# Where the products of a step stand between scores and sums, and when their outputs are turned, in the first pass of a two-layer attention kernel

## Chip, cores and metric

One core of one Trainium2 chip. The metric is the device time of one execution in microseconds (us), of which the median of several runs is given. All data are 32-bit floats.

## What is computed

Two layers on x of shape 8 x 256 x 64 x 64. The first is attention with keys and values from a 4x4 strided convolution (so 4096 queries against 256 keys, 8 heads of 32), the second linear attention over q, k, v and a 5x5 depthwise copy of them. The part that matters here, cut from the reference:

```
xr = layernorm(conv4x4_stride4(x, w_sr));  q = w_q x;  k, v = split(w_kv xr)
attn = softmax(q k^T * 32**-0.5)           # per head, over 256 keys
x2 = x + gamma * w_out (attn v)            # end of layer 0
qkv = w_qkv x2                             # layer 1 starts: 768 x 256 on 4096 columns
...                                        # depthwise 5x5, relu attention, projection
```

## The kernel before, in words

The kernel has three passes: the first computes layer 0 and the qkv of layer 1 and stores them to DRAM, the second the sums and the 5x5 branch, the third the output. Only `first_pass` (L575) changes.

**Steps.** The first pass is a loop over n (L991) of 256 steps and some more that empty the pipeline. A step is one (image b, strip s of 512 columns, half c of the heads, half kc of the keys): 32 steps an image, 4 a strip. With m = n - 1, a step n holds for TensorE:

- `scores` (L770) of n: four products, one a head, each on 32 rows of the array ("32x512" in the profile, line L774), into four PSUM banks. ScalarE takes each out with an exponential (L780) into a tile `e`.
- `valued` (L786) of m: four products on 32 columns of the array (L791) of `e` with the values, into the bank `av`.
- after both key halves, so in even n, `counted` (L804): four products of ones with the sum of the two halves' `e` (L807), into the bank `den`. The sum of the halves is made by GpSimd (POOL) in `joined` (L800, L802): four additions in odd n, **in place over the `e` of the first half**. They therefore wait until `valued` of that first half, which stands in the same odd step, has read it; and `counted` in the step after waits for all four.
- in even n, `queries` (L756): the q of the next two steps (two products of the full array, L759); `normed` (L809): `att` times the reciprocal of `den`, by two transposes on VectorE (DVE), and on ScalarE two checks over 512 columns each, which write back to the bank `den` (L823, L824).
- in steps 12 to 25 of an image, parts of `keys_values` (L675) of the next image (`ahead`): two taps of the convolution a step (L687), then the layernorm and k and v.
- what `todo` holds for n: `added` (L827: the output projection of a strip, L831, and its sum into x, L832, in n = 2 and 6 modulo 8), `differences` (L841, n = 2 modulo 8), and the products of `qkv` (L860).

**The products of qkv.** A pair of strips is done with seven products instead of eight (Strassen-Winograd) for each of three pairs of weights, in the order 1, 2, 0: p1, p2, p6, p7, p4, p5, p3, 21 in 8 steps, one bank each. In the steps 3, 4, 5, 6, 7, 0, 1 modulo 8 there are 4, 3, 4, 0, 3, 4, 3 of them. `ended` (L882) makes an output of a product on DVE (`part_whole`, L891); for pairs 1 and 2 it then transposes it at once (`turned`, L894) and, for pair 1, copies it on ScalarE to `stage` (L893). For pair 0 the sum goes straight to `stage` (L888). `stored` (L899) sends both to DRAM through SP's queue.

**Banks.** Scores, q, the output projection and the qkv products share five banks (`bank`, L591). A scores step takes four of them, in turn, so its last three wait until the three products that stand fourth, third and second ahead of it have been taken out of their banks, mostly by DVE. `av`, `den` and the convolution have a bank each.

**Order.** Every engine runs its instructions in one order, which a planner sets when the program is built: it goes by the order of the code, but puts a later instruction first where it holds the earlier one not ready at that time. `tc.keep_in_program_order` pins an instruction behind all that was traced for its engine before it. Each product of the code becomes two TensorE instructions.

Of the kernel before, what the change touches and what calls it, by code (L numbers as in the profile page):

```python
# [27 lines left out]
F32 = mybir.dt.float32  # L28
AF = mybir.ActivationFunctionType
ALU = mybir.AluOpType  # L30
AX = mybir.AxisListType

P = 128
# [541 lines left out]
def first_pass(ctx: ExitStack, tc: tile.TileContext, a, fine, planes, x2d, kd, vd, wtd):  # L575
# [207 lines left out]

    sums = {}

    def valued(b, s, c, kc, es):  # L786
        if kc == 0:
            sums["av"] = psum_early.tile([P, QB], F32, tag="av", name=f"av_{b}_{s}_{c}")
        for h in range(4):
            cols = slice(h * D0, (h + 1) * D0)  # L790
            nc.tensor.matmul(  # L791
                sums["av"][cols],
                vvs[b][:, kc, c * P + h * D0 : c * P + (h + 1) * D0],
                es[h],
                start=(kc == 0),
                stop=(kc == 1),
            )
# [11 lines left out]
    def normed(b, s, c):  # L809
        av, den = sums["av"], sums["den"]  # L810
        i = 2 * ((b * NG + s) * 2 + c)
        att = rest.tile([P, QB], F32, tag="att", name=f"att_{b}_{s}_{c}", bufs=4)
        r = rest.tile([P, NB, D0], F32, tag="rden", name=f"rden_{b}_{s}_{c}", bufs=1)
        one = two.tile([P, NB], F32, tag="one", name=f"one_{b}_{s}_{c}")
        nc.scalar.copy(att, av)

        nc.vector.transpose(r.rearrange("p n d -> p (n d)"), den)
        nc.vector.reciprocal(one, r[:, :, 0])
        r = rest.tile([P, NB, D0], F32, tag="rall", name=f"rall_{b}_{s}_{c}", bufs=1)
        nc.vector.transpose(r, one.unsqueeze(2).to_broadcast([P, NB, D0]))  # L820
        r = r.rearrange("p n d -> p (n d)")
        nc.vector.tensor_mul(att, att, r)
        nc.scalar.activation(den, den, AF.Copy, accum_out=seen[:, i : i + 1])  # L823
        nc.scalar.activation(den, r, AF.Copy, accum_out=seen[:, i + 1 : i + 2])  # L824
        return att

    def added(b, s, att, oc):  # L827
# [23 lines left out]
        quarters[b, g] = b11, b21, b22, t1, t2, t3, t4  # L851

    def new_stage(b, g, j):
        st = rest.tile([P, 4, NB + 1, NB + 1], F32, tag=f"stage{j}", name=f"stage_{b}_{g}_{j}", bufs=1)
        nc.gpsimd.memset(st[:, :, 0 if g // 2 else NB], 0.0)
        nc.gpsimd.memset(st[:, :, :, 0 if g % 2 else NB], 0.0)
        return st


    def qkv(b, g, pair):  # L860
        js = 2 * pair, 2 * pair + 1
        b11, b21, b22, t1, t2, t3, t4 = quarters[b, g]
        w = consts["wqkv"].rearrange("p c (j r o) -> p c j r o", j=3, r=2)[:, :, pair]
        s1, s2, s3, s4 = (combined[:, pair, i] for i in range(4))
        name = f"{b}_{g}_{pair}"
        stages = [new_stage(b, g, j) for j in js] if pair < 2 else None
        turned = None
        if pair:
            turned = [
                rest.tile([P, NB // 2, 4, D0], F32, tag=f"turned{j}", name=f"turned_{b}_{g}_{j}", bufs=1) for j in js  # L870
            ]

        def product(i, w, x):
            ps = bank(f"qkv_{name}_{i}")
            nc.tensor.matmul(ps, w, x, start=True, stop=True)  # L875
            return ps

        def part(i, bufs=1):
            return halves.tile([P, QB], F32, tag=f"part{i}", name=f"part_{name}_{i}", bufs=bufs)


        def ended(r, h, u, ps, op=ALU.add):  # L882
            if stages:
                y, x = g // 2, g % 2
                inside = stages[r][:, 2 * h : 2 * h + 2, y : y + NB, x : x + NB]
            rows = lambda t: t.rearrange("p (f y x) -> p f y x", f=2, y=NB)
            if not turned:
                nc.vector.tensor_tensor(inside, rows(u), rows(ps), op)  # L888
                return
            whole = part("whole", 2)  # L890
            nc.vector.tensor_tensor(whole, u, ps, op)  # L891
            if stages:
                nc.scalar.copy(inside, rows(whole))  # L893
            nc.vector.transpose(  # L894
                turned[r][:, :, 2 * h : 2 * h + 2].rearrange("p y f e -> p f y e"),
                whole.rearrange("p (f y e) -> p f y e", f=2, y=NB // 2),
            )

        def stored(r):  # L899
            j = js[r]  # L900
            if stages:
                nc.sync.dma_start(
                    planes[b, j].rearrange("g (k i f) e -> g k i (f e)", k=4, i=D1)[:, g],
                    stages[r].rearrange("p f y x -> p (f y x)"),
                )
            if not turned:
                return
            for k in range(4):
                n, src = 4 * (j % 2) + k, turned[r][k * D0 : (k + 1) * D0].rearrange("p y f e -> p y (f e)")
                if j < 4:  # L910
                    dst = kd[b][n].rearrange("a (y w) x b e -> a b (w x) y e", w=2)
                    nc.sync.dma_start(dst[g // 2, g % 2], src)
                else:
                    dst = vd[b][n][1 : NB2 + 1, 1 : NB2 + 1]
                    dst = dst.rearrange("(y w a) (x b) e -> a b w x y e", w=2, a=2, b=2)
                    for w in range(2):
                        nc.sync.dma_start(dst[g // 2, g % 2, w], src[w * NB : (w + 1) * NB])


        u = {}  # L920

        def p1():
            ps = product(1, w[:, 0, 0], b11)
            u[1] = part(1)
            nc.scalar.copy(u[1], ps)

        def p2():
            ended(0, 0, u[1], product(2, w[:, 1, 0], b21))

        def p6():  # L930
            u[2] = part(2)
            nc.vector.tensor_add(u[2], u[1], product(6, s2, t2))

        def p7():
            u[3] = part(3)
            nc.vector.tensor_add(u[3], u[2], product(7, s3, t3))

        def p4():
            ended(1, 0, u[3], product(4, w[:, 1, 1], t4), ALU.subtract)

        def p5():
            ps = product(5, s1, t1)
            ended(1, 1, u[3], ps)
            u[4] = part(4)
            nc.vector.tensor_add(u[4], u[2], ps)
            stored(1)

        def p3():
            ended(0, 1, u[4], product(3, s4, b22))
            stored(0)  # L950

        return [p1, p2, p6, p7, p4, p5, p3]

# [16 lines left out]
    q, es, att = {0: first}, {}, {}  # L970
    ahead = iter(())

    def outputs(b, s):
        return [lambda oc=oc: added(b, s, [att[b, s, 0], att[b, s, 1]], oc) for oc in range(2)]

    def qkv_lazy(b, g, pair):
        made = []

# [9 lines left out]

    n_all = len(order)
    todo = {}  # L990
    for n in range(n_all + 14):  # L991
        m = n - 1
        if n < n_all:
            b, s, c, kc = order[n]
            es[n] = scores(b, s, c, kc, q[n // 2])
        if 0 <= m < n_all:
            valued(*order[m], es[m])
            if order[m][3] == 1:
                counted(*order[m][:3], es.pop(m - 1))
                es.pop(m)  # L1000
                att[order[m][:3]] = normed(*order[m][:3])
        if n < n_all and kc == 1:
            joined(es[n - 1], es[n])
        if n < n_all and kc == 0 and n + 2 < n_all:
            q.pop(n // 2 - 1, None)
            q[n // 2 + 1] = queries(*order[n + 2][:3])
        if n >= 6 and (n - 6) % 8 == 4 and (n - 6) // 4 < B * NG:

            b, s = (n - 6) // 4 // NG, (n - 6) // 4 % NG
            work = [outputs(b, s) + [lambda b=b, s=s: differences(b, s // 2)]]  # L1010
            products = [p for pair in (1, 2, 0) for p in qkv_lazy(b, s // 2, pair)]
            for i in (4, 3, 4, 0, 3, 4, 3):
                work.append(products[:i])
                products = products[i:]
            for i, w in enumerate(work):
                todo.setdefault(n + i, []).extend(w)
        elif n >= 6 and (n - 6) % 8 == 0 and (n - 6) // 4 < B * NG:
            todo.setdefault(n, []).extend(outputs((n - 6) // 4 // NG, (n - 6) // 4 % NG))
        next(weights, None)
        if n < n_all:  # L1020
            b, at = n // 32, n % 32
# [2 lines left out]
            if b + 1 < B:  # L1024
# [6 lines left out]
                    next(ahead)  # L1031
                elif at >= 20:
                    next(ahead, None)
        for f in todo.pop(n, ()):
            f()
    for _ in weights:
        pass

# [3 lines left out]
    total = bank("total")[:, :2]  # L1042
    nc.tensor.matmul(total, mean_w, both, start=True, stop=True)
    fits = const.tile([P, 4], F32, tag="fits", name="fits")
    nc.vector.tensor_scalar(fits[:, 0:1], total[:, 0:1], SUM_MAX / C, None, ALU.is_le)
    nc.vector.tensor_scalar(fits[:, 1:2], total[:, 1:2], INVERSE_MAX / C, None, ALU.is_le)
    nc.vector.tensor_mul(fits[:, 2:3], fits[:, 0:1], fits[:, 1:2])
    nc.vector.tensor_copy(fine, fits[:, 2:3])

# [674 lines left out]
```

## Time and profile before

| what | value |
|---|---|
| median of 10 runs | 4056.96 us (4053.03 to 4063.7) |
| time of the profiled execution | 4055.02 us |
| its span, first to last instruction | 4053.2 us |
| last scores product of the first pass | starts at 2118.68 us |
| TensorE (PE) busy in the span | 3982.0 us, 98% |
| DVE / ScalarE / GpSimd busy | 2261.3 / 1645.5 / 1275.1 us |
| granted TensorE clock | 0.993 of full speed |

The timeline of the trace gives for each row its start, its length, the engine, the line, the operation, the tiles (written <- read), and in brackets how long the engine was idle before it and what ended that. TensorE's matmuls overlap, so their lengths add to more than the time; the distance from one start to the next is what a product takes.

### The profile page before, as it was taken

What the parts mean: (1) busy time and instruction counts of PE and PEld (TensorE: products, weight loads), DVE (VectorE), ACT (ScalarE), POOL (GpSimd) and SP (SyncE); (2) the same over time, 40 slices, a digit from 0 to 9 for tenths busy, and PEclk for the clock granted to TensorE, in tenths of its full rate; (3) what the DMA queues carried; (4) which work ended last, traced back from release to release, by engine and by line L of the source; (5) the groups of instructions that cost most, each with busy time, mean ns of one, the idle gap of its engine ahead of it and who ended that gap; (6) DMA issues with size and microseconds to landing.
All of it is one profiled execution on the core that took longest, in us unless ns stands there. A gap on an engine that the chain in (4) does not pass through costs nothing. (4 is left out here: it accounts for less than half of the span.)

```text
span 4053.2 us, 70276 instructions
## 1 busy us (share of the span) xinstructions
PE 3982.0 (98%) x27074; PEld 2316.2 (57%) x27074; DVE 2261.3 (56%) x3752; ACT 1645.5 (41%) x3473; POOL 1275.1 (31%) x1394
## 2 busy tenths in 40 slices
PE   8999999999999999999998999999999998999999
PEld 4443434434334344343336888888888886556555
DVE  2576455564655545546665566666666665444443
ACT  3345354453544544535552222222222223454444
POOL 2234333343332433423443444434434441000000
PEclk9999999999999999999999999999999999999999
DMA  7655445445354453544549878778777656777674
GB/s 239 189 179 159 125 97 143 100 97 152 91 143 104 98 135 103 136 109 103 135 102 244 246 226 233 220 224 233 220 223 234 204 171 174 232 199 233 196 235 137
DMA packets 569897, 691.37 MB, mean 171 GB/s; under 512 B 60112, under 2 KB 429264, under 8 KB 565328
## 3 DMA queue, kind: packets, MB, share of 16 engines
q1 hardware_dynamic: 569552, 686.78, 60.7%
q8 instruction: 215, 3.52, 0.4%
q14 instruction: 130, 1.06, 0.1%
HBM read 412.54 MB, written 274.10 MB: 169 GB/s over the span
## 5 line engine op out<-in xcount | busy, mean ns | idle before, releaser
L802 POOL TENSOR_TENSOR e<-e,e 128x512 f32<-128x512 f32 x512 | 658.1, 1318 | 938.8 <-PE av L791 923.4
L780 ACT ACTIVATE e<-sc 128x512 f32<-128x512 f32 x1024 | 532.8, 601 | 709.0 <-PE sc L774 709.0
L774 PE MATMUL sc<-q,kk 32*128 32x512 f32 x2048 | 418.5, 640 | 7.2 <-DVE part_whole L891 3.9
L1180 PE MATMUL cv<-w,c 128*128 128x128 f32 x3072 | 385.7, 279 | 6.8 <-POOL c L1124 6.8
L1180 PEld LDWEIGHTS cv<-w,c 128*128 128x128 f32 x3072 | 359.9, 192 | 36.3 <-issue 28.8
L1547 DVE TENSOR_TENSOR y<-z,xs 128x256 f32<-128x256 f32 x256 | 142.6, 645 | 313.6 <-ACT z L1538 295.3
L1222 PE MATMUL sums<-vq,r 128*32 128x288 f32 x4096 | 306.6, 412 | 0.0
L891 DVE TENSOR_TENSOR part_whole<-part,qkv 128x512 f32<-128x512 f32 x256 | 170.7, 670 | 219.9 <-PE qkv L875 216.1
L774 PEld LDWEIGHTS sc<-q,kk 32*128 32x128 f32 x2048 | 130.0, 183 | 278.0 <-issue 140.3
L875 PE MATMUL qkv<-differences,combined 128*128 128x512 f32 x576 | 278.6, 592 | 0.8 <-DVE differences L848 0.8
L1196 ACT ACTIVATE r<-s 128x512 f32<-128x512 f32 x256 | 160.5, 627 | 291.8 <-DVE s L1195 288.3
L791 PE MATMUL av<-e,vv 128*32 128x512 f32 x2048 | 275.5, 608 | 0.0
L1538 ACT ACTIVATE z<-p,bn 128x256 f32<-128x256 f32 x256 | 133.9, 578 | 315.0 <-PE p L1529 208.5
L759 PE MATMUL q<-x,wq 128*128 128x512 f32 x512 | 255.3, 621 | 0.0
L1184 PE MATMUL cv<-c,w 128*128 128x128 f32 x2048 | 253.4, 277 | 0.0
L1529 PE MATMUL p<-att,wproj 128*128 128x512 f32 x512 | 249.4, 609 | 1.9 <-ACT att L1512 1.9
L1187 ACT COPY both<-cv 128x512 f32<-128x512 f32 x128 | 75.1, 586 | 432.7 <-PE cv L1180 374.3
L687 PE MATMUL sr<-x,wsr 128*128 128x256 f32 x1024 | 236.9, 385 | 11.5 <-DMA wsr<-in_w_sr_dram 11.5
L1529 PE MATMUL p<-agg,wproj 128*128 128x512 f32 x512 | 241.3, 594 | 0.0
L1184 PEld LDWEIGHTS cv<-c,w 128*128 128x128 f32 x2048 | 239.7, 192 | 0.0
L687 PEld LDWEIGHTS sr<-x,wsr 128*128 128x128 f32 x1024 | 192.8, 191 | 76.5 <-issue 40.2
L831 PE MATMUL o<-att,wout 128*128 128x512 f32 x512 | 231.8, 593 | 0.0
(143 smaller groups left out, 6202.3 us busy)
## 6 DMA issues: line engine op xcount, KB each, us to landing
vq<-v SPq DMA_DIRECT2D x256, 384.0 KB
planes<-stage SPq DMA_DIRECT2D x128, 578.0 KB
d<-planes SPq DMA_DIRECT2D x128, 578.0 KB
raw<-planes SPq DMA_DIRECT2D x128, 272.0 KB
x<-in_xp_dram SPq DMA_DIRECT2D x64, 512.0 KB
wsr<-in_w_sr_dram SPq DMA_DIRECT2D x128, 256.0 KB
x<-x SPq DMA_DIRECT2D x128, 256.0 KB
k<-turned SPq DMA_DIRECT2D x256, 128.0 KB
```

Source lines behind the costliest of these rows:

```text
L687: nc.tensor.matmul(ps[:, oc], w[:, ci, oc * P : (oc + 1) * P], xt[:, ci, f * NK : (f + 1) * NK], start=(f == ci == oc == 0), stop=(f == R ...
L759: nc.tensor.matmul(ps, consts["wq"][:, ci, c * P : (c + 1) * P], x_tiles[b][:, ci, s * QB : (s + 1) * QB], start=(ci == 0), stop=(ci == 1),)
L774: nc.tensor.matmul(scs[h], kks[b][rows, c, kc * P : (kc + 1) * P], qs[rows], start=True, stop=True)
L780: nc.scalar.activation(e, scs[h], AF.Exp, scale=D0**-0.5)
L791: nc.tensor.matmul(sums["av"][cols], vvs[b][:, kc, c * P + h * D0 : c * P + (h + 1) * D0], es[h], start=(kc == 0), stop=(kc == 1),)
L802: nc.gpsimd.tensor_tensor(es0[h], es0[h], es1[h], ALU.add)
L831: nc.tensor.matmul(ps, consts["wout"][:, c, oc * P : (oc + 1) * P], att[c], start=(c == 0), stop=(c == 1))
L875: nc.tensor.matmul(ps, w, x, start=True, stop=True)
L1180: nc.tensor.matmul(out, x, m, start=(da == 0), stop=(da == 1))
L1184: nc.tensor.matmul(out, m, x, start=(da == 0), stop=(da == 1))
L1222: nc.tensor.matmul(ps[h * D0 : (h + 1) * D0, : 36 * D1].rearrange("p (r n e) -> p r n e", r=3, e=D1), kt[:, par, h, 2 * r + c], vq[:, r : ...
L1529: nc.tensor.matmul(ps.rearrange("p (f q n) -> p f q n", f=4, q=4), wproj[:, j, oc * P : (oc + 1) * P], src, start=(j == 0), stop=(j == 3),)
```

## The change

1. **Turns a step later.** In `ended` the transpose and the copy to `stage` are put in a list `late`, and so is `stored` for pairs 1 and 2. The list is run in the next step, after that step's `scores`, and its instructions are pinned to the order of the code. `whole` gets 6 buffers instead of 2.
2. **Checks.** In `normed` the two 512-column checks become two 16-column ones, over the column `turn[:, :, 0]` and over `one`, also run late; they no longer write to `den`. The two limits are divided by 32 to match.
3. **Order in a step.** `added` and `differences` come behind `queries` and `normed`, in the step in which they were. The products of qkv come ahead of `queries`. In odd steps except 13 to 25 of an image (`last`) they come **ahead of `valued`**, directly behind `scores`; in the others behind `valued` and `counted`, and the convolution's part comes after them.
4. **Counts.** The products in steps 3, 4, 5, 6, 7, 0, 1 modulo 8 are 2, 3, 4, 1, 4, 3, 4.
5. **Tiles.** `stage` has two slots for four tiles (tag `j % 2`).

The core of the diff:

```
-            whole = part("whole", 2)
+            whole = halves.tile([P, QB], F32, tag="whole", name=f"whole_{name}_{r}_{h}", bufs=6)
             nc.vector.tensor_tensor(whole, u, ps, op)
-            if stages:
-                nc.scalar.copy(inside, rows(whole))
-            nc.vector.transpose(
...
+            def turn():
+                tc.keep_in_program_order(
+                    nc.vector.transpose(
...
+                if stages:
+                    tc.keep_in_program_order(nc.scalar.copy(inside, rows(whole)))
+
+            late.append(turn)
...
+        def ready(r):
+            if turned:
+                late.append(lambda: stored(r))
+            else:
+                stored(r)
...
-        nc.scalar.activation(den, den, AF.Copy, accum_out=seen[:, i : i + 1])
-        nc.scalar.activation(den, r, AF.Copy, accum_out=seen[:, i + 1 : i + 2])
+
+        def noted():
+            for k, t in enumerate((turn[:, :, 0], one)):
+                copy = two.tile([P, NB], F32, tag="copy", name=f"copy_{b}_{s}_{c}_{k}")
+                tc.keep_in_program_order(
+                    nc.scalar.activation(copy, t, AF.Copy, accum_out=seen[:, i + k : i + k + 1])
+                )
+
+        late.append(noted)
...
-        st = rest.tile([P, 4, NB + 1, NB + 1], F32, tag=f"stage{j}", name=f"stage_{b}_{g}_{j}", bufs=1)
+        st = rest.tile([P, 4, NB + 1, NB + 1], F32, tag=f"stage{j % 2}", name=f"stage_{b}_{g}_{j}", bufs=1)
...
             es[n] = scores(b, s, c, kc, q[n // 2])
+        was, late[:] = list(late), []
+        for f in was:
+            f()
+
+
+        last = n < n_all and kc == 1 and not 12 <= n % 32 <= 25
+        if last:
+            for f in todo.pop(n, ()):
+                f()
         if 0 <= m < n_all:
             valued(*order[m], es[m])
             if order[m][3] == 1:
                 counted(*order[m][:3], es.pop(m - 1))
                 es.pop(m)
-                att[order[m][:3]] = normed(*order[m][:3])
-        if n < n_all and kc == 1:
-            joined(es[n - 1], es[n])
+        for f in todo.pop(n, ()):
+            f()
         if n < n_all and kc == 0 and n + 2 < n_all:
             q.pop(n // 2 - 1, None)
             q[n // 2 + 1] = queries(*order[n + 2][:3])
...
+        if 0 <= m < n_all and order[m][3] == 1:
+            att[order[m][:3]] = normed(*order[m][:3])
+        if n < n_all and kc == 1:
+            joined(es[n - 1], es[n])
+        if n >= 6 and (n - 6) % 4 == 0 and (n - 6) // 4 < B * NG:
             b, s = (n - 6) // 4 // NG, (n - 6) // 4 % NG
...
+                for i, count in enumerate((2, 3, 4, 1, 4, 3, 4)):
+                    todo[n + 1 + i] = products[:count]
+                    products = products[count:]
         next(weights, None)
...
-        for f in todo.pop(n, ()):
-            f()
```

More of the change, by code (lines that the diff above doesn't have):

```diff
@@ L784, in first_pass @@
     sums = {}
+    late = []
     def valued(b, s, c, kc, es):
@@ L812, in normed @@
         att = rest.tile([P, QB], F32, tag="att", name=f"att_{b}_{s}_{c}", bufs=4)
-        r = rest.tile([P, NB, D0], F32, tag="rden", name=f"rden_{b}_{s}_{c}", bufs=1)
+        turn = rest.tile([P, NB, D0], F32, tag="rden", name=f"rden_{b}_{s}_{c}", bufs=1)
         one = two.tile([P, NB], F32, tag="one", name=f"one_{b}_{s}_{c}")
         nc.scalar.copy(att, av)
-        nc.vector.transpose(r.rearrange("p n d -> p (n d)"), den)
-        nc.vector.reciprocal(one, r[:, :, 0])
+        tc.keep_in_program_order(nc.vector.transpose(turn.rearrange("p n d -> p (n d)"), den))
+        nc.vector.reciprocal(one, turn[:, :, 0])
         r = rest.tile([P, NB, D0], F32, tag="rall", name=f"rall_{b}_{s}_{c}", bufs=1)
@@ L876, in product, with part @@
             return ps
-        def part(i, bufs=1):
-            return halves.tile([P, QB], F32, tag=f"part{i}", name=f"part_{name}_{i}", bufs=bufs)
+        def part(i):
+            return halves.tile([P, QB], F32, tag=f"part{i}", name=f"part_{name}_{i}", bufs=1)
         def ended(r, h, u, ps, op=ALU.add):
@@ L889, in ended @@
                 return
-            whole = part("whole", 2)
+            whole = halves.tile([P, QB], F32, tag="whole", name=f"whole_{name}_{r}_{h}", bufs=6)
             nc.vector.tensor_tensor(whole, u, ps, op)
-            if stages:
-                nc.scalar.copy(inside, rows(whole))
-            nc.vector.transpose(
-                turned[r][:, :, 2 * h : 2 * h + 2].rearrange("p y f e -> p f y e"),
-                whole.rearrange("p (f y e) -> p f y e", f=2, y=NB // 2),
-            )
+            def turn():
+                tc.keep_in_program_order(
+                    nc.vector.transpose(
+                        turned[r][:, :, 2 * h : 2 * h + 2].rearrange("p y f e -> p f y e"),
+                        whole.rearrange("p (f y e) -> p f y e", f=2, y=NB // 2),
+                    )
+                )
+                if stages:
+                    tc.keep_in_program_order(nc.scalar.copy(inside, rows(whole)))
+            late.append(turn)
         def stored(r):
@@ L945, in p5 @@
             nc.vector.tensor_add(u[4], u[2], ps)
-            stored(1)
+            ready(1)
         def p3():
             ended(0, 1, u[4], product(3, s4, b22))
-            stored(0)
+            ready(0)
         return [p1, p2, p6, p7, p4, p5, p3]
@@ L971, in first_pass @@
     ahead = iter(())
-    def outputs(b, s):
-        return [lambda oc=oc: added(b, s, [att[b, s, 0], att[b, s, 1]], oc) for oc in range(2)]
     def qkv_lazy(b, g, pair):
@@ L990, in first_pass @@
     todo = {}
-    for n in range(n_all + 14):
+    for n in range(n_all + 16):
         m = n - 1
@@ L1006, in first_pass @@
             q[n // 2 + 1] = queries(*order[n + 2][:3])
-        if n >= 6 and (n - 6) % 8 == 4 and (n - 6) // 4 < B * NG:
-            b, s = (n - 6) // 4 // NG, (n - 6) // 4 % NG
[L1010 to L1018, printed above, removed]
+        if 0 <= m < n_all and order[m][3] == 1:
[3 more added lines that the diff above has]
+        if n >= 6 and (n - 6) % 4 == 0 and (n - 6) // 4 < B * NG:
+            b, s = (n - 6) // 4 // NG, (n - 6) // 4 % NG
+            for oc in range(2):
+                added(b, s, [att[b, s, 0], att[b, s, 1]], oc)
+            if s % 2:
+                differences(b, s // 2)
+                products = [p for pair in (1, 2, 0) for p in qkv_lazy(b, s // 2, pair)]
+                for i, count in enumerate((2, 3, 4, 1, 4, 3, 4)):
+                    todo[n + 1 + i] = products[:count]
+                    products = products[count:]
         next(weights, None)
@@ L1044, in first_pass @@
     fits = const.tile([P, 4], F32, tag="fits", name="fits")
-    nc.vector.tensor_scalar(fits[:, 0:1], total[:, 0:1], SUM_MAX / C, None, ALU.is_le)
-    nc.vector.tensor_scalar(fits[:, 1:2], total[:, 1:2], INVERSE_MAX / C, None, ALU.is_le)
+    nc.vector.tensor_scalar(fits[:, 0:1], total[:, 0:1], SUM_MAX / D0 / C, None, ALU.is_le)
+    nc.vector.tensor_scalar(fits[:, 1:2], total[:, 1:2], INVERSE_MAX / D0 / C, None, ALU.is_le)
     nc.vector.tensor_mul(fits[:, 2:3], fits[:, 0:1], fits[:, 1:2])
```

## Prediction

> **What bounds the kernel now.** First the page: TensorE is busy for 98% of the span, and the last scores product of the first pass starts at 2118.68 us, so this pass is half the time and is a row of TensorE products without holes of any length. Every wait of TensorE there is time of the kernel; ScalarE, DVE and GpSimd (POOL) at 41, 56 and 31% are paid only where TensorE waits for them.
>
> ```profile
> PE 3982.0 (98%) x27074; PEld 2316.2 (57%) x27074; DVE 2261.3 (56%) x3752; ACT 1645.5 (41%) x3473; POOL 1275.1 (31%) x1394
> ...
> L802 POOL TENSOR_TENSOR e<-e,e 128x512 f32<-128x512 f32 x512 | 658.1, 1318 | 938.8 <-PE av L791 923.4
> ```
>
> The second line is `joined`: 1.3 us an addition, four in two steps, and POOL's wait ahead of them is for `valued` (av). Then the waits of the stretch from 60 to 2120 us, TensorE's weight loads alone, which stand for the products behind them:
>
> ```profile
> PEld sc L774 <- DVE part L945: 47.3, 81, 1.6
> PEld sc L774 <- ACT stage L893: 43.2, 57, 0.8
> ...
> PEld den L807 <- POOL e L802: 30.4, 65, 2.7
> ...
> PEld sc L774 <- DVE part_whole L891: 17.0, 18, 2.0
> PEld sc L774 <- DVE part L932: 15.9, 60, 1.0
> ```
>
> Scores wait for a bank that DVE has still to empty: this is what can be won. Part of a weight load's idle time goes by while products still run, so I size the loss from starts: scores to valued is 1.07 us at the least in the timeline, and what is over that is the wait. In images 2 to 8 it is 0.50, 1.03, 0.50, 1.03 and 0.57 us in the steps 4, 5, 6, 0 and 2 modulo 8 and none in 1, 3, 7: 3.63 us in 8 steps, 101.6 in the 28 such groups, and 108.4 with what is more in steps 22 and 24 of an image. The first image has 25.4, of it 4.8 before its step 11. Sum 133.7 us.
>
> Third, two pieces of the timeline. Steps 37 and 38, as most are:
>
> ```profile
> 356.63 2.17 PE L774 MATMUL sc<-q,kk 32*128 32x512 f32 x8
> ...
> 358.74 1.07 PE L791 MATMUL av<-e,vv 128*32 128x512 f32 x8
> ...
> 359.73 1.98 PE L875 MATMUL qkv<-x,wqkv 128*128 128x512 f32 x4
> ...
> 359.93 4.94 POOL L802 TENSOR_TENSOR e<-e,e 128x512 f32<-128x512 f32 x4 [8.12 <-PE av L791]
> ...
> 361.55 1.88 PE L875 MATMUL qkv<-differences,combined 128*128 128x512 f32 x4
> ...
> 363.36 1.64 PE L774 MATMUL sc<-q,kk 32*128 32x512 f32 x8
> ...
> 364.93 1.07 PE L791 MATMUL av<-e,vv 128*32 128x512 f32 x8
> ```
>
> The first row is a stalled scores step (356.63 to 358.74, 2.11 us). Then valued releases POOL 1.19 us after its start, POOL adds until 364.87, and `counted` can follow valued at 365.81 without waiting: **four qkv products, 3.63 us, cover POOL**. Steps 5 and 6, where there are no qkv products yet:
>
> ```profile
> 77.82 1.06 PE L791 MATMUL av<-e,vv 128*32 128x512 f32 x8
> ...
> 78.82 1.90 PE L774 MATMUL sc<-q,kk 32*128 32x512 f32 x8
> ...
> 79.02 6.46 POOL L802 TENSOR_TENSOR e<-e,e 128x512 f32<-128x512 f32 x4 [5.21 <-PE av L791]
> ...
> 80.65 1.06 PE L791 MATMUL av<-e,vv 128*32 128x512 f32 x8
> ...
> 81.53 1.09 PE L807 MATMUL den<-e,ones_w 128*32 128x512 f32 x4
> ...
> 85.53 1.05 PE L807 MATMUL den<-e,ones_w 128*32 128x512 f32 x2 [1.69 <-POOL e L802]
> 86.50 1.98 PE L759 MATMUL q<-x,wq 128*128 128x512 f32 x4
> ```
>
> Valued, scores, valued, counted with nothing of the full array between: counted takes 4.97 us from its start to the next product instead of 0.97, and q, which needs nothing of POOL, stays behind it: the planner did not move it up. The same is seen in steps 2, 4, 8 and 10.
>
> **What the Trainium skill says.** "TensorEngine Tiling (Array Packing)", Key Properties: changing the tiling mode drains TensorE. The trace agrees: scores to valued (rows to columns) takes 1.07 us, valued to counted (same mode) 0.88. Same page, Gotcha 1 (PSUM Pressure): different row tiles write different banks; here four of five banks a step, hence the waits above. "TensorE: Matmul & The Clock Gate", Part 3, The mechanism: matmuls are not reordered on the engine. Agrees: q stands behind the waiting counted at 86.50.
>
> **The change, part by part.**
>
> *Qkv products ahead of valued in odd `last` steps.* It moves what covers POOL to the wrong side: POOL is released only by valued, and between valued and counted there are now scores and valued alone. From the start of valued: release 1.20 us (358.74 to 359.93), four additions, mean 1293 ns in the steady part (330 to 2115 us), 5.17, then 1.02 from POOL's end to the product behind counted (85.48 to 86.50): 7.39 us. Without a wait it is 1.00 + 1.07 + 0.88 + 0.97 = 3.92. **Wait 3.47 us** a time. Nothing else in those steps can shorten it, since the additions wait for valued alone; behind counted stand, on TensorE, qkv, q, output projection and all later steps. How often: `last` holds in 9 odd steps of an image (1 to 11 and 27 to 31), 72 in all; in steps 1, 3, 5, 7, 9 of the first there is no product to move and the wait is there already. 67 x 3.47 = 232.5, less what four of those places (steps 12, 28, 32, 256) wait already, 0.79 + 1.09 + 0.24 + 1.58 = 3.7: **+229**. In the last image, step 19 has no convolution behind it and only 2 products: about +2. Bounds of a wait: four additions take 4.94 us at best and 5.41 at worst in steady steps, so 3.24 to 3.71.
>
> *Scores free of DVE.* Turns (0.71 us each) no longer stand between the outputs, and behind the last products there is now valued (1.00 us), q (1.8), the convolution (3.45) or the output projection (3.5). DVE needs 0.65 to 0.69 us an output, two for p5, against 0.86 a product: for p7, p4, p5, p3 the last bank needed, p5's, comes free some 4.1 us after the first product starts, while scores begin at 3.5 + 1.0. What is left: step 24 (only 0.55 us between) and the last image's steps 14 to 26, some 8 us; in the first image DVE's weight products (1.9 us each) still stand in the way, of 20.6 I take half. 108.4 - 8 + 10: **-110** (bounds -95 and -125).
>
> *Switches of mode* in a `last` step: before scores-valued-full-scores, after scores-full-valued-scores, three each. Full to columns is not in the trace; nearest 0.1 (full to rows) to 0.2 (rows to columns): 0, between -7 and +7 over 72 steps.
>
> *Small checks.* Away: 0.58 + 0.19 + 0.60 + 0.19 us of ScalarE, 128 times; come: two copies of 16 columns, not shown; from copies of 512 (0.59) and 256 (0.37) columns some 0.15 to 0.25 plus 0.19 each. About 100 us of ScalarE time, hidden by its 59% idle; nobody waits for it: 0. If that cover were gone, 0.8 us a place.
>
> *Turns and stores a step later.* The same instructions; on ScalarE the copies (0.62) come behind the exponentials. On SP each store's one plane and 4 or 8 token DMAs move behind the next step's; queued behind them are x2 stores and convolution weights, for which TensorE waits 5.3 us today. 0, bounds -5 and +10.
>
> *Two `stage` slots.* POOL's memsets wait for the other pair's store. A store issued at 1030.34 lets the memset at 1034.90 go, 4.6 us later; between one pair's store and the other's memset lies at least a step of 8 us. 0, bound +10 (a memset ahead of the additions lengthens the wait above).
>
> **Sum**: 4055.0 (profiled) - 110 + 229 + 2 = 4176; the median lies 1.9 above the profiled time: **4178**. With the bounds (-125 + 214 to -95 + 248, and the small ones) 4140 to 4225.
>
> **Rivals.** (1) *The planner moves full-array products in front of counted*, where it holds POOL late. For it: it does reorder (a convolution tap between two output products in step 50). Against it: it left q behind counted in five steps of the same pattern. Then the wait is covered by qkv and q, and only the gain is left: 4057 - 110 = **3947**, faster. It decides from 3.47 us of work put there; at 1.8 us in all 67 places gain and loss are even. (2) *It moves one product*, 0.86 us: 67 x 2.61 - 3.7 - 110 = +61: **4118**. (3) *The scores' waits stay* because pinned turns now stand at the head of DVE's queue: +229 and no gain, **4288**. Against it: TensorE's new waits give DVE time. (4) Waits and gains cancel otherwise: 4057.
>
> **Chances.** Forecast 0.74, (1) 0.14, (2) 0.06, (3) 0.03, (4) 0.03. Faster by over 0.2% (about what a measurement of this kernel can tell from no change) 0.15; within 0.03; slower 0.82. The forecast's own range with (2) and slack for the planner's order gives 4090 to 4250; outside lie (1), (3) and a little of the forecast.
>
> **What would show it.** Right: scores to valued or to qkv at 1.07 us nearly everywhere; counted to the next product 4.4 us (0.97 + 3.47) in 67 even steps, with POOL named as releaser, 0.97 in steps 14 to 26; waits of counted for POOL about 230 us in all. Wrong: qkv or q products between valued and counted (rival 1 or 2), scores still waiting for DVE (3), waits for DMA in the first pass, or additions much off 1.29 us.

## The result, and the profile after

The changed kernel takes **4182.7 us** (median of 8 runs, 4179.58 to 4187.68) against 4056.9 us before (28 runs): 1.031 times as long, 95% interval 1.0301 to 1.0319. The forecast was 4178. The profiled execution, of 4186.6 us, has a span of 4184.8 us, 131.6 more than before.

The page after, with the lines for TensorE, for the additions of `joined` and for `counted`:

```profile
span 4184.8 us, 70247 instructions
...
PE 4076.1 (97%) x27074; PEld 2309.5 (55%) x27074; DVE 2242.2 (54%) x3752; ACT 1516.8 (36%) x3473; POOL 1271.5 (30%) x1394
...
L804 POOL TENSOR_TENSOR e<-e,e 128x512 f32<-128x512 f32 x512 | 654.3, 1310 | 897.0 <-PE av L793 897.0
...
L809 PE MATMUL den<-e,ones_w 128*32 128x512 f32 x1024 | 333.7, 608 | 35.8 <-POOL e L804 33.8
```

TensorE is busy for 97%, and yet the time is 3% longer: its busy time rose by 94.1 us (3982.0 to 4076.1) with the same 27074 instructions, so much of the waiting counts as busy and this line can't show the loss. The waits of the first pass can (60 to 2245 us; waited for, us in all, times, longest):

```profile
POOL stage L864 <- DMA planes<-stage: 314.9, 80, 14.5
...
PEld den L809 <- POOL e L804: 225.2, 275, 2.6
...
PEld sc L774 <- ACT copy L830: 18.4, 22, 0.8
...
PEld sc L774 <- DVE whole L901: 10.7, 16, 2.5
...
PEld sc L774 <- DVE part L967: 6.3, 7, 3.4
```

Before, the weights of `counted` waited 30.4 us for GpSimd; now 225.2. Those of the scores waited 47.3 and 15.9 us for the two kinds of `part` and 17.0 for `part_whole`; now 6.3 for `part` and 10.7 for `whole`. The 18.4 us put down to the small checks (`copy`, L830) are no loss of that size: ahead of the first weight load of most scores steps stands an idle of some 0.8 us, while products still run. These 22 are the steps 4, 12 and 28 of an image (and step 20 of the last), which lose 0.2 us each by their starts. The timeline of one step with products ahead of `valued`:

```profile
650.74 1.07 PE L793 MATMUL av<-e,vv 128*32 128x512 f32 x8
...
651.74 1.14 PE L774 MATMUL sc<-q,kk 32*128 32x512 f32 x8
651.93 4.96 POOL L804 TENSOR_TENSOR e<-e,e 128x512 f32<-128x512 f32 x4 [11.41 <-PE av L793]
...
652.81 1.06 PE L793 MATMUL av<-e,vv 128*32 128x512 f32 x8
...
653.69 1.85 PE L809 MATMUL den<-e,ones_w 128*32 128x512 f32 x4
...
655.72 1.04 PE L809 MATMUL den<-e,ones_w 128*32 128x512 f32 x2 [0.18 <-POOL e L804]
...
656.95 1.05 PE L809 MATMUL den<-e,ones_w 128*32 128x512 f32 x2 [0.18 <-POOL e L804]
...
657.93 1.12 PE L885 MATMUL qkv<-differences,combined 128*128 128x512 f32 x2
```

Here scores follow `valued` without a wait (652.81 - 651.74 = 1.07), which was the aim. But GpSimd is released by the `valued` at 650.74, 1.19 us after its start, adds until 656.89, and between that `valued` and `counted` TensorE has only scores and one more `valued`. `counted` takes 657.93 - 653.69 = 4.24 us where 0.97 would do.

Summed over the first pass from starts, as in the prediction: "scores' wait" is what a scores group takes beyond 1.07 us until the next group starts, "counted's wait" what `counted` takes beyond 0.97, "pass" the time from the first scores product to the last, "behind" the time from there to the end of the span. A delay of the start of `counted`, or of other products, is in neither column of waits. The columns come from the one profiled execution of each kernel, and executions of one kernel lie up to some 13 us apart (before: 4052.05 to 4064.63), so a few us in them decide nothing. All in us:

| kernel | median | pass | scores' wait | counted's wait | behind |
|---|---|---|---|---|---|
| before | 4056.9 | 2067.0 | 133.9 | 19.9 | 1934.5 |
| after | 4182.7 | 2178.8 | 34.8 | 228.9 | 1952.6 |

So the time went to `counted` (+209.0) and to the stretch behind the last scores (+18.1); the scores gave back 99.1, and the first scores start 1.7 us later.

### The profile page after: what moved, and what is told of

The parts are those of the page before. It is cut to its first block, busy times and chain, and to the rows that moved or that the text cites. A ratio compares the mean times of both kernels' runs of the same rounds, so it can differ in the third digit from the quotient of the medians.

```text
span 4184.8 us, 70247 instructions
## 1 busy us (share of the span) xinstructions
PE 4076.1 (97%) x27074; PEld 2309.5 (55%) x27074; DVE 2242.2 (54%) x3752; ACT 1516.8 (36%) x3473; POOL 1271.5 (30%) x1394
## 3 DMA queue, kind: packets, MB, share of 16 engines
q8 instruction: 215, 3.52, 0.4%
## 5 line engine op out<-in xcount | busy, mean ns | idle before, releaser
L809 PE MATMUL den<-e,ones_w 128*32 128x512 f32 x1024 | 333.7, 608 | 35.8 <-POOL e L804 33.8
L774 PE MATMUL sc<-q,kk 32*128 32x512 f32 x2048 | 324.1, 641 | 4.8 <-DVE part L967 3.0
L885 PE MATMUL qkv<-differences,combined 128*128 128x512 f32 x576 | 304.6, 620 | 1.0 <-DVE differences L857 1.0
L759 PE MATMUL q<-x,wq 128*128 128x512 f32 x512 | 245.3, 601 | 0.0
L767 ACT COPY q<-q 128x512 f32<-128x512 f32 x128 | 75.1, 586 | 457.0 <-PE q L759 457.0
L901 DVE TENSOR_TENSOR whole<-part,qkv 128x512 f32<-128x512 f32 x256 | 175.3, 687 | 121.8 <-PE qkv L885 66.6
```

What stands on the lines that cost most here:

```text
L759: nc.tensor.matmul(ps, consts["wq"][:, ci, c * P : (c + 1) * P], x_tiles[b][:, ci, s * QB : (s + 1) * QB], start=(ci == 0), stop=(ci == 1),)
L774: nc.tensor.matmul(scs[h], kks[b][rows, c, kc * P : (kc + 1) * P], qs[rows], start=True, stop=True)
L809: nc.tensor.matmul(sums["den"][h * D0 : (h + 1) * D0], ones_w, es[h], start=True, stop=True)
```

## Experiments

Twelve kernels. Theory A (the prediction's): full-array products ahead of `valued` leave nothing to cover GpSimd, and this alone is the loss. Its rivals were that something else in the new order or in the late turns costs the time, and that the gain at the scores has another cause than supposed. The table holds them all; each median is of several runs timed in turn with the kernel before on the same chip, to which its ratio refers.

| kernel | median | ratio to before, interval | pass | scores' wait | counted's wait | behind |
|---|---|---|---|---|---|---|
| e1_valued_first | 4039.1 | 0.9949 (0.9932-0.9966) | 2031.5 | 49.7 | 68.6 | 1955.8 |
| e2_sums_apart | 4033.9 | 0.9936 (0.9919-0.9952) | 2027.4 | 34.1 | 76.6 | 1952.6 |
| e3_two_sums_on_dve | 4120.2 | 1.0151 (1.0134-1.0168) | 2112.0 | 48.2 | 121.0 | 1952.6 |
| e4_last_alone | 4239.4 | 1.0447 (1.0429-1.0464) | 2240.9 | 93.0 | 233.0 | 1941.1 |
| e5_turn_at_once | 4181.1 | 1.0297 (1.0283-1.0311) | 2177.4 | 34.7 | 230.7 | 1949.9 |
| e6_more_in_odd_steps | 3995.2 | 0.9847 (0.9834-0.9861) | 1994.2 | 47.1 | 35.6 | 1946.7 |
| e7_late_turns_alone | 4061.7 | 1.0010 (1.0002-1.0019) | 2065.4 | 106.3 | 37.5 | 1948.3 |
| e8_difference_on_dve | 3988.8 | 0.9829 (0.9816-0.9842) | 1985.9 | 49.0 | 24.5 | 1950.6 |
| e9_four_stages_at_once | 4061.5 | 1.0010 (1.0001-1.0018) | 2073.0 | 64.7 | 89.1 | 1935.9 |
| e11_after_four_stages | 4174.5 | 1.0288 (1.0274-1.0302) | 2179.6 | 35.4 | 232.2 | 1941.3 |
| e12_memsets_behind_adds | 4010.4 | 0.9884 (0.9867-0.9900) | 2020.2 | 84.5 | 20.3 | 1935.6 |
| e13_late_four_stages | 3977.9 | 0.9800 (0.9786-0.9813) | 1982.6 | 48.6 | 21.4 | 1936.0 |

### The place of the products

**e4_last_alone**: the kernel before, and only this added ahead of `valued`:

```
+        if n < n_all and kc == 1 and not 12 <= n % 32 <= 25:
+            for f in todo.pop(n, ()):
+                f()
         if 0 <= m < n_all:
             valued(*order[m], es[m])
```

> The kernel before with one part of the change alone: in the same odd steps the qkv products stand ahead of valued. Theory: counted then waits about 3.27 us in 67 places, +215 us, and the scores behind those steps win some 0.5 to 1.0 us each, -43 us: about 4229 us. Rival (the loss comes from the late turns, the small checks, the counts or the shared slots): 4057 within 15, or less.

Measured 4239.4 us. From the second image on `counted` waits 3.12 to 3.26 us in nearly all of the same nine steps of an image, 233.0 us in all, and the scores keep 93.0. The weights of `counted` name GpSimd (60 to 2300 us; before 30.4, see above):

```profile
PEld den L807 <- POOL e L802: 228.0, 278, 2.6
```

This one part is the loss, and larger than that of the whole change.

**e1_valued_first**: the reverse, the kernel after without that part, so that the products of every step stand behind the sums:

```
-        last = n < n_all and kc == 1 and not 12 <= n % 32 <= 25
-        if last:
-            for f in todo.pop(n, ()):
-                f()
```

> The changed kernel, but the qkv products stand behind valued in every odd step, as they did before. Theory (counted waits for GpSimd because nothing but scores and valued lies between the release of its additions and counted): the wait of 3.27 us goes where 3 or 4 products lie between and is about 1.3 us where there are only 2 (steps 3, 11, 27 of an image, 24 places, 31 us); scores standing directly behind p7, p4, p5, p3 wait some 0.57 us again (4 places an image, 18 us). 4183 - 209 + 31 + 18 = about 4023 us, faster than the kernel before. Rival (the loss comes from the pinned order of DVE, the shared stage slots or the stores): within 20 us of 4183.

Measured 4039.1 us, **143.6 below the kernel after and 0.5% below the one before**. Six of the nine waits of an image are gone; 2.0 to 2.2 us stay in steps 4, 12 and 28, which made it 16 us slower than expected (1.3 us was forecast there). The timeline of steps 131 and 132 (3 and 4 modulo 32) shows why:

```profile
1114.57 1.78 POOL L858 TENSOR_TENSOR differences<-x 128x512 f32<-128x512 f32 x1 [8.26 <-DVE x L841]
1114.70 1.07 PE L793 MATMUL av<-e,vv 128*32 128x512 f32 x8
1115.70 1.98 PE L885 MATMUL qkv<-x,wqkv 128*128 128x512 f32 x4
...
1116.62 2.64 POOL L804 TENSOR_TENSOR e<-e,e 128x512 f32<-128x512 f32 x2
...
1119.78 1.91 PE L809 MATMUL den<-e,ones_w 128*32 128x512 f32 x6
...
1121.96 1.05 PE L809 MATMUL den<-e,ones_w 128*32 128x512 f32 x2 [0.27 <-POOL e L804]
```

In this step there are only two qkv products, and on GpSimd the third difference (1.78 us) and the memsets of `stage` stand ahead of the additions, which begin 1.92 us after the start of `valued` and not 1.19.

**e6_more_in_odd_steps** and **e8_difference_on_dve** take the two reasons in turn:

```
-                for i, count in enumerate((2, 3, 4, 1, 4, 3, 4)):
+                for i, count in enumerate((4, 2, 4, 1, 4, 2, 4)):
```
```
-        nc.gpsimd.tensor_tensor(t3, b22, b12, ALU.subtract)
+        nc.vector.tensor_sub(t3, b22, b12)
```

> The kernel with every product of a step behind the valued and counted products (4039 us), and the qkv products dealt out 4, 2, 4, 1, 4, 2, 4 in place of 2, 3, 4, 1, 4, 3, 4, so that the step before each wait of 2.0 to 2.2 us holds four products and not two. Theory that the counted products wait because too little work of TensorE lies between the scores and them: 24 waits of 2.1 us go, 4039 - 50 = about 3989. Rival, that those waits come from the differences and memsets ahead of the adds on GpSimd and only move: 4030 to 4040.

> The kernel with 4, 2, 4, 1, 4, 2, 4 products, and the third difference computed on VectorE, not on GpSimd ahead of the four adds. If GpSimd's chain still ends last in steps 4, 12 and 28, some 24 waits of 0.5 to 1.5 us go: 10 to 35 us below the kernel it is made from. If four products already cover it: no difference (within 5 us). If VectorE's longer chain holds back the qkv products: up to 15 us slower.

With four products in every odd step 3995.2 us, 43.9 less, as the theory had it (about 3989); what is left in steps 4, 12 and 28 is 0.7. With the difference on VectorE too, 3988.8: counted's wait falls by 11.1 us more, the time by 6.4, less than the 10 to 35 expected, since the products already covered most of it.

### The chain on GpSimd

**e2_sums_apart**: the order of the kernel after, but the sums go to a tile of their own, so that the additions wait for the exponentials of the second half, and no longer for `valued` of the first:

```
-            nc.gpsimd.tensor_tensor(es0[h], es0[h], es1[h], ALU.add)
+            t = two.tile([P, QB], F32, tag="both", name=f"both_{n}_{h}", bufs=4)
+            nc.gpsimd.tensor_tensor(t, es0[h], es1[h], ALU.add)
```

`counted` reads these tiles. To make room `e` has 10 buffers and `whole` 5.

> The changed kernel with its order kept, but the four additions write tiles of their own, so that they no longer wait for valued to have read the first half (10 instead of 12 exponential tiles and 5 instead of 6 outputs make room). Theory: GpSimd starts with the exponentials, some 1.8 us after the start of the odd step's scores, and is done 6.8 after it; with 4 products counted would come at 7.65, no wait; with 2 products a wait of about 0.9, 24 times. 4183 - 209 + 21 = about 3995 us. Rival (counted waits because GpSimd is busy or slow, or the loss is elsewhere): 4183 within 30.

Measured 4033.9 us: 148.8 below the kernel after **in the same order of products**. Of the 210.5 us that `counted` waits behind step 10 in the kernel after, some seven tenths are gone, so the order is harmful mainly together with the addition in place. It is 39 us above the expectation: 2.3 us stay in steps 4, 12 and 28, where 0.9 was expected, again with the third difference ahead of the additions.

**e3_two_sums_on_dve**: every second addition on VectorE.

```
-            nc.gpsimd.tensor_tensor(es0[h], es0[h], es1[h], ALU.add)
+            (nc.gpsimd if h % 2 else nc.vector).tensor_tensor(es0[h], es0[h], es1[h], ALU.add)
```

> The changed kernel, but two of the four additions run on VectorE (DVE), two on GpSimd, still in place. Theory: the wait is the length of GpSimd's chain, so it falls by two additions, 2.47 us, in 67 places: 4183 - 165 = about 4018 us, if DVE takes its two (0.7 us each) without being late. Rival (the wait is set by the release from valued or by DVE's queue): between 4100 and 4183.

A miss: 4120.2 us, 102 above the expectation and within the range of the rival. The timeline of a step like the one shown of the kernel after:

```profile
653.09 3.52 POOL L804 TENSOR_TENSOR e<-e,e 128x512 f32<-128x512 f32 x2 [3.93 <-PE av L793]
653.09 2.37 DVE L804 TENSOR_TENSOR e<-e,e 128x512 f32<-128x512 f32 x2
...
654.80 2.90 PE L809 MATMUL den<-e,ones_w 128*32 128x512 f32 x8
```

Half the additions did not take half the time: GpSimd's two took 3.52 us (1.76 each; four took 4.96, 1.24 each, in the kernel after), VectorE's two 2.37 (0.69 and 1.77, where it takes 0.69 alone). The wait fell with GpSimd's chain, from 4.96 to 3.52 us, and so to 1.7 to 1.9 us, but no further. VectorE's queue has a part in it as well: the column of `counted` falls by 107.9 us, but the pass only by 66.8. The scores wait 13.4 us more, `counted` starts 14 us later after `valued` (nearly all of it in the first image; its products waited 28.5 us for additions on VectorE), and the qkv products and output projections take some 10 us more.

### The late turns, and what empties the banks

**e7_late_turns_alone**: the first half of the change (late turns and stores, small checks, six `whole`, two `stage`), with the loop's order and counts of the kernel before. **e5_turn_at_once**: the reverse, the kernel after with

```
-            late.append(turn)
+            turn()
...
-            if turned:
-                late.append(lambda: stored(r))
-            else:
-                stored(r)
+            stored(r)
```

> The first half of the change alone: late turns and stores, small checks, six buffers of whole, two stages, with the loop's order and the dealing of products of the kernel before. If the scores' waits end because the turns are late: they fall from 188.5 us to about 110, counted stays at its 34 us, the tail costs 10 to 18 us more: 4057 - 79 + 14 = about 3992. If they end because of the order: 4057 plus the tail, about 4070.

> The kernel after, but the turns of the qkv outputs and their stores run at once, not in the step that follows; the small checks and the new order stay. First theory: the late turns are what empties the banks in time for the scores, and they also send the last stores of the first pass later. The order alone (the kernel before with the products put ahead in the same steps) left 147.6 us of waits in the scores' groups against 92.4 in the kernel after, so some 55 us come back and up to 18 us of the tail go: 4183 + 55 - 18 = about 4220. Rival: the new order alone takes the scores' waits away and the late turns only cost the tail: about 4165.

The first theory fell in both; the rival came within 8 and 16 us. Late turns alone: 4061.7 us, within 0.2% of before. The scores' waits fall by 27.6 us, but counted's rise by 17.6, the products behind `valued` start 9 us later, and the stretch behind the last scores grows by 13.8 (in a profiled execution that was the slowest of 13, 4068.2 us). Without late turns the kernel after takes 4181.1 us, and its scores wait as little as with them (34.7 and 34.8). So in the kernel after **the new order gives the gain at the scores without the late turns, and these give nothing in sum**: they cost 8 us in the first two images and gain some 1.2 in each later one. The counts and the small checks are new in e5 too and were not tested apart. The likely reason, not tested by itself: valued, q and the output projection, which now stand between the qkv products and the scores, and the waits of `counted` leave VectorE time enough to turn at once. What the rival had wrong in e5 is the stretch behind the last scores, which stayed 15.4 us longer than before although nothing is late: 1949.9 us.

### Two slots of stage, and a memset at the head of a queue

**e11_after_four_stages** is e5 with `stage` in four slots and `whole` in two buffers as before; **e9_four_stages_at_once** makes the same edits to e8 (so turns at once, four slots).

```
-        st = rest.tile([P, 4, NB + 1, NB + 1], F32, tag=f"stage{j % 2}", name=f"stage_{b}_{g}_{j}", bufs=1)
+        st = rest.tile([P, 4, NB + 1, NB + 1], F32, tag=f"stage{j}", name=f"stage_{b}_{g}_{j}", bufs=1)
```

> The kernel after with the turns and stores at once, two buffers of whole and four slots of stage. Against the kernel with the turns at once and two slots (4181 us) the slots and the buffers of whole alone differ. If two slots are what delays the stretch behind the last scores: 4181 - 14 = about 4167. Rival, that the products left over and the waits of the counted products make that stretch longer: 4181.

> The kernel with 4, 2, 4, 1, 4, 2, 4 products behind the sums and the third difference on VectorE (3989 us), with the turns and stores at once, two buffers of whole and four slots of stage, as in the kernel before; so only the new order and the small checks are left of the change. If the stretch behind the last scores is some 14 us longer because two stage slots make its outputs wait for stores, and the order of q behind the qkv products is what takes the scores' waits away: 3989 - 14 = about 3975. If the late turns are needed in this order: the scores' waits go up by 30 to 55 us, to 4005 to 4030. If neither matters: 3989.

e11: the stretch behind the last scores is 8.6 us shorter than in e5 (1949.9 to 1941.3), the pass 2.2 longer; 4174.5 us, a gain of half of what was expected. With e4, which has slots and turns of before and 1941.1 us there, the +18.1 of the kernel after splits: 6.6 for the order (e4 less before), 8.6 for the slots (with the buffers of `whole`), 2.7 for the late turns and stores. Of the 6.6, 2.9 is a longer wait of the last `counted` (it takes 5.45 us in e4, 2.55 before); the rest is not explained. The 2.7 is not clear of what one execution differs from another.

e9 was a miss: 4061.5 us, outside all three cases. Behind the last scores it gains 14.7 us, as expected, but `counted` waits 64.6 us more than in e8, some 2.7 to 3.0 us in steps 6, 22 and 30 of most images. Its timeline at step 133:

```profile
1145.22 1.07 PE L793 MATMUL av<-e,vv 128*32 128x512 f32 x8
...
1149.14 0.52 SPq L918 DMA_DIRECT2D planes<-stage  x1
...
1149.55 0.16 POOL L864 MEMSET stage<- 128x68 f32 x1 [10.59 <-DMA planes<-stage]
...
1149.88 4.95 POOL L804 TENSOR_TENSOR e<-e,e 128x512 f32<-128x512 f32 x4
...
1151.92 1.57 PE L809 MATMUL den<-e,ones_w 128*32 128x512 f32 x4
```

The additions could begin at about 1146.4 (1.19 us after `valued`); they begin at 1149.88, because on GpSimd a memset of 0.16 us stands in front of them and waits 10.59 us for a store. In e8, with the late turns, this memset stands behind the additions.

**e12_memsets_behind_adds** is e9 with that put right:

```
-        nc.gpsimd.memset(st[:, :, 0 if g // 2 else NB], 0.0)
-        nc.gpsimd.memset(st[:, :, :, 0 if g % 2 else NB], 0.0)
+        tc.keep_in_program_order(nc.gpsimd.memset(st[:, :, 0 if g // 2 else NB], 0.0))
+        tc.keep_in_program_order(nc.gpsimd.memset(st[:, :, :, 0 if g % 2 else NB], 0.0))
...
+        if n < n_all and kc == 1:
+            joined(es[n - 1], es[n])
         for f in todo.pop(n, ()):
             f()
...
-        if n < n_all and kc == 1:
-            joined(es[n - 1], es[n])
```

> The kernel with the turns at once and four stages (4062 us), with the four adds of an odd step traced ahead of its qkv products and the memsets of stage pinned to the order of the code on GpSimd, so that no memset waiting for a store stands ahead of adds. If that is what costs 64.6 us at the counted products there: 4062 - 65 = about 3997, and down to 3975 if the scores' waits shrink with it to those of the kernel with late turns. If the turns between the outputs are what costs (DVE later at every bank): it stays above 4040.

4010.4 us: counted's wait is back at 20.3 us, that of the kernel before, so memsets ahead of the additions were the cause. The time is 13 us above the expected 3997, since the scores' wait rose from 64.7 to 84.5 us as that of `counted` went; e8 with late turns has 49.0.

**e13_late_four_stages** brings the good parts together: e8 with four slots, adds and memsets ordered as in e12, late turns, three buffers of `whole` and 11 of `e`.

> The kernel with late turns, 4, 2, 4, 1, 4, 2, 4 products behind the sums and the third difference on VectorE (3989 us), with four slots of stage, three buffers of whole and 11 of e to make room, and the adds traced ahead of the products with the memsets pinned behind them. If the two costs are apart (two slots make the stretch behind the last scores 14 us longer, turns between the outputs cost the scores 35 us): 3989 minus 9 to 14, about 3977. If three buffers of whole or 11 of e hold the exponentials or outputs back: 3995 to 4020.

**3977.9 us**, 0.98 of before (0.9786 to 0.9813), the best of all. Its weights of `counted` still name GpSimd in the first pass (60 to 2050 us):

```profile
PEld den L809 <- POOL e L804: 24.1, 36, 2.6
```

But of its 21.4 us at `counted`, 20.0 fall up to step 10 of the first image, before there are qkv products. e12 and e13 differ in the late turns and in the buffers of `whole` (2 and 3) and `e` (12 and 11) that these need: the scores' wait is 84.5 against 48.6 us. So late turns, with the third buffer of `whole` that was not tested apart, are worth some 36 us where TensorE doesn't wait elsewhere, and nothing where (kernel after, e5) it stands at `counted` anyway.

## Why the prediction came out right, and where its steps were off

**Counted's wait: right in mechanism and place, 22 us too large.** Forecast 3.47 us in 67 places and +231; measured +209.0. In the 66 of these places that lie in the pass the mean is 3.14 us: 2.99 to 3.27 in 61 of them, and 0.9 to 5.2 in steps 12, 28, 30, 32 and 34, as the first image ends. 4.24 us a `counted`, 0.97 in nearly all of steps 14 to 26, GpSimd as releaser, 2.2 us in step 20 of the last image: as announced. The mis-sized term is the four additions, taken as 4 x 1.293 = 5.17 us from these steady steps of before (330 to 2115 us; the second line is the kernel after, 330 to 2230 us):

```profile
L802 POOL TENSOR_TENSOR e<-e,e 128x512 f32<-128x512 f32 x444 | 559.7, 1293 | 797.9 <-PE av L791 797.9
L804 POOL TENSOR_TENSOR e<-e,e 128x512 f32<-128x512 f32 x444 | 550.4, 1273 | 775.8 <-PE av L793 775.8
```

The records of two additions in a row overlap a little, so four times their mean length is more than four take: the busy time gives 559.7 / 111 = 5.04 us before and 550.4 / 111 = 4.96 after. So 0.13 of the 0.21 us too much is the overlap. More than half of the other 0.08 comes from 12 of the 111 groups of before, which took 5.4 us while VectorE made a difference of two SBUF tiles; in the kernel after only one group met that. The lower bound, 4.94, would have been the better value. In steps 4, 12 and 28 the wait is 0.2 less again, because the scores wait there for as long themselves.

**Scores free of VectorE: right within 11 us, its cause half wrong.** Forecast -110 (bounds -95 and -125), measured -99.1. From the third image on 2.0 us an image are left (3.1 in the last); the first keeps 13.4 us (forecast about 15) and the second 8.4, which the forecast gave nothing extra. The step named the late turns first, then what stands behind the last products; e5 shows that the new order does it without the late turns. Rival (3), waits that stay because pinned turns stand at the head of VectorE's queue, did not come. The reason given against it, that TensorE's new waits give VectorE time, fits e5, but isn't needed: e13 has late turns and hardly any of these waits, and keeps only 48.6 us.

**What was put at nothing.** *Stage slots*: forecast 0, bound +10; measured 8.6 us, and not at the additions but behind the last scores, where the forecast had costed no stretch at all. The argument there ("at least a step of 8 us" between one pair's store and the other's memset) did not hold for GpSimd, whose memsets waited 314.9 us for stores (136.1 before), once for 14.5. It cost `counted` little in this order of the queue: in 118 of 128 steps the additions begin 1.2 us after `valued`, and never later than 2.0. In e9, in another order, 23 begin 4.1 to 4.9 us after it. *Late turns and stores*: 0, bound +10, measured 2.7 us behind the last scores, not clear of the spread. *Small checks*: ScalarE's busy time fell by 128.7 us (1645.5 to 1516.8; forecast about 100), and the forecast of no gain was not tested by itself: the trace before names the old checks as releaser of only 6.7 us of idle of TensorE's weights in the pass. A copy took 0.23 to 0.25 us and its sum 0.22, near the bounds set. *Left out altogether*: the order's own 6.6 us behind the last scores.

**The sum.** +121 forecast, +131.6 between the profiled spans: -99.1 + 209.0 + 18.1 + 1.7 and some 2 of small ones. One term was 11 us too good and one 22 too bad, the stretch behind the last scores made up the rest, and the profiled execution lies 3.9 us above the median; so 4178 against 4182.7 is in part luck, while the sign and the range rest on the wait that was there to be read.

**Rivals (1) and (2)**, that the planner moves full-array products between `valued` and `counted`, did not happen, but for once: in step 28 of the first image three qkv products and one of q came in front of `counted`, which then waited 1.28 us. In all later steps with products ahead of `valued`, until the last scores, only scores and the second `valued` stand there. What (1) priced at 3947 us is nearly the case of e13, where full-array products stand there by the program's order: 3977.9 us, with 48.6 us of waits left at the scores.

## What to carry to other kernels

Count what lies between an engine's release and the product that needs its result: here 3.6 us of qkv products between `valued` and `counted` were cover for GpSimd, and moving them one place up laid bare some 3.2 us in nine of the 32 steps of an image. Look for the narrower chain before reordering: the addition in place tied GpSimd to `valued`, and a tile of its own (e2) took some seven tenths of the wait away in the same order. When an instruction that waits for a DMA shares a queue with a short chain that TensorE needs, put it behind that chain on purpose; memsets of 0.16 us cost some 65 us in all in e9.

## What the runs showed of the hardware

VectorE and GpSimd, both adding two SBUF tiles, hold each other up. The Trainium skill, "SBUF — State Buffer", section "SBUF: two separate sides", says that an operation of VectorE with two SBUF inputs and one of GpSimd that reads SBUF take a shared port pair in turn, the other being blocked meanwhile. e3 agrees: in 28 of its steps both begin their two additions together, and in each of these VectorE's first takes 0.65 to 0.69 us, as alone, GpSimd's first ends 1.13 us after it, VectorE's second 0.55 after that, and GpSimd's second again 1.13 later, 3.5 us in all. One that was held up needs about 0.1 us less from then on than it takes alone (0.69 and 1.24), so turns cost a little less than the sum, 2 x 0.69 + 2 x 1.24 = 3.86; freely side by side it would have been 2.48. Splitting such a chain over the two engines gained 1.44 us of 4.96, and not half.
